# A graph layer on one core: in the gather stage the other engines wait for a drain behind each group of matmuls, and its buffers get fixed places

## The chip, the cores and the metric

The kernel runs on one core of a Trainium2 chip. A core has five engines that run side by side, each with its own queue in program order: PE (matrix multiplication), DVE (vector), ACT (scalar), POOL and SP. They tell each other of finished work by semaphores, which are counters: an instruction adds to one when it has ended, and another waits until it has reached a value. Matmuls write into PSUM, which has eight banks; everything else lies in SBUF. Transfers are done by 16 DMA engines; SP and ACT give them whole transfers, and POOL gives them gathers by an index. The metric is the time of one execution on the device in microseconds (us).

## The reference

12,500 nodes have 256 features each in `x`, and 200,000 edges go from `src` to `dst`, sorted by `dst`. Each node gets the sum of its neighbours' normalized features, two dense layers with a batch normalization each, and its own `x` back:

```python
h = jnp.maximum(_layernorm(x, axis=-1), 0.0)
agg = jax.ops.segment_sum(h[src], dst, num_segments=N)
z = (1.0 + eps_gin) * h + agg
t = jax.nn.relu(_batchnorm(jnp.dot(z, W1) + b1, g1, bt1))
out = jax.nn.relu(_batchnorm(jnp.dot(t, W2) + b2 + h, g2, bt2))
return x + out
```

Everything is float32; W1 is 256x512 and W2 512x256.

## The kernel before, in words

A short start brings the indices into columns and tests whether the fast path may be taken (lines 92 to 220). The fast path has three stages. The **gather stage** (lines 298 to 493) makes `h`, sums it over the edges and does the first layer. The second reads the first layer's result back, normalizes it and does the second layer (500 to 522). The third does the last normalization and adds `x` (527 to 549). Between stages stands the sum of a batch normalization's statistics, which needs all nodes. Only the gather stage is changed.

It works on two grids. Nodes lie in 25 chunks of 512 (`CH`), the last of 212. Edges lie in 1563 tiles of 128, in 131 groups of 12 tiles (`GT`); since edges are sorted by `dst`, the 1536 edges of a group reach fewer than 128 neighbouring nodes. The loop at line 472 takes one group per step:

- `gather(i + 4)` (377): POOL issues 12 indirect transfers (line 382), one for each tile: 128 rows of 256 features into a place `gt` of a ring of five (`AHEAD + 1`). For the first 24 groups (`LEAD`) the rows come from `x`, since `h` isn't ready, and `settle` (322) normalizes them in place on DVE and ACT (lines 328 to 339). Later ones come from the table `h_tab`. Within a group the last tile is fetched first.
- `sums(i)` (403): DVE makes one-hot matrices `oh` that say which edge belongs to which of the group's nodes (407), and PE adds up the 12 tiles in one bank `ps` with 12 matmuls (417). A float32 matmul is two passes in the profile, so a group has 24.
- `join(i - 1)` (422): ACT copies the sum of the group before out of PSUM, `zs` (424), and DVE makes a second one-hot matrix `at` that says at which columns it belongs (426).
- `put(i - 1)` (431): two matmuls (four passes) turn and place that sum in `pz` (436). `pz` has one place, two banks wide.
- `add(i - 1)` (441): DVE adds `pz` to the chunk's `zc` (449), which SP has loaded from the table `h_cols` (395) and ACT has scaled by 1 + eps (396).
- When a chunk is complete, `first_layer` (452): eight matmuls with W1, in pairs, each into a bank `ph` (458), their statistics on DVE (462) and a copy on ACT (463), which is then stored (464).

In the first 20 steps `h_chunk` (354) is called as well: it loads a chunk of `x`, normalizes it, stores it to `h_tab`, turns it with transposes on PE (365) into the bank `pc` and stores it to `h_cols`.

The order of each engine's queue is made by the framework's scheduler, from the order of the calls and its own estimates of time. Places and waits are made by it too: a pool with n buffers hands out n places in turn, and the next user of a place waits for all that used it. Each group of matmuls adds to PE's counter when its last matmul has ended, and ACT, DVE, POOL and SP wait for values of that counter: `zs` and the `oh` two groups on wait for `ps`; `add` waits for `pz`; the statistics wait for `ph`; and the first gather of a group waits for the matmuls of five groups earlier, which read the same place of the ring.

In the built program PE's queue stands so in the middle of the stage, as far as one group goes: the last ten matmuls of `ps(i)`, the first two of `ps(i+1)`, the two of `pz(i)`, the other ten of `ps(i+1)`.

Of the kernel before, what the change touches and what calls it, by code (L numbers as in the profile page):

```python
# [14 lines left out]
P = 128  # L15
# [14 lines left out]
def kernel(  # L30
# [233 lines left out]
    def fast():  # L264
# [24 lines left out]
        with ExitStack() as fs:  # L289
# [8 lines left out]
            with ExitStack() as es:  # L298
                ln = es.enter_context(tc.tile_pool(name="ln", bufs=2))
                gat = es.enter_context(tc.tile_pool(name="gat", bufs=AHEAD + 1))  # L300
                sel = es.enter_context(tc.tile_pool(name="sel", bufs=2))
                zcp = es.enter_context(tc.tile_pool(name="zc", bufs=4))
                tsp = es.enter_context(tc.tile_pool(name="ts", bufs=2))
                ps_h = es.enter_context(tc.tile_pool(name="ps_h", bufs=1, space=PSUM))
                ps_i = es.enter_context(tc.tile_pool(name="ps_i", bufs=1, space=PSUM))
                ps_s = es.enter_context(tc.tile_pool(name="ps_s", bufs=2, space=PSUM))
                ps_z = es.enter_context(tc.tile_pool(name="ps_z", bufs=1, space=PSUM))
                ps_t = es.enter_context(tc.tile_pool(name="ps_t2", bufs=2, space=PSUM))
# [13 lines left out]
                def settle(v, pairs, rows, to, tag):  # L322
# [15 lines left out]
                    for c in reversed(range(rows)):  # L338
                        nc.scalar.activation(  # L339
                            to[:, c, :], v[:, c, :], AF.Relu, bias=nb[:, c : c + 1], scale=rs[:, c : c + 1]  # L340
                        )

# [11 lines left out]
                def h_chunk(g):  # L354
# [3 lines left out]
                    ht = ln.tile([P, R, D], F32, name="ht")  # L358
                    settle(xts.pop(g), -(-slots // 2), slots, ht, "c")
                    carry(nc.scalar, ht, h_tab, g, store=True)  # L360
                    hc = ln.tile([P, DC, CH], F32, name="hc")
                    for d in range(DC):
                        ph = ps_h.tile([P, CH], F32, name="pc")
                        for c in range(slots):
                            nc.tensor.transpose(  # L365
                                ph[:, c * P : (c + 1) * P], ht[:, c, d * P : (d + 1) * P], ident
                            )
                        if d % 2:
                            nc.scalar.copy(hc[:, d, :n], ph[:, :n])
                        else:  # L370
                            nc.vector.tensor_copy(hc[:, d, :n], ph[:, :n])  # L371
                    nc.sync.dma_start(h_cols[g, :, :, :n], hc[:, :, :n])

                groups = [(t0, min(GT, NTILE - t0)) for t0 in range(0, NTILE, GT)]
                gathered = {}

                def gather(i):
                    t0, n = groups[i]
                    ga = gat.tile([P, GT, D], F32, name="gt")
                    for t in reversed(range(t0, t0 + n)):  # L380
                        rows = left if t == full_tiles else P
                        nc.gpsimd.indirect_dma_start(  # L382
                            out=ga[:rows, t - t0, :], out_offset=None, in_=x if i < LEAD else h_tab,
                            in_offset=bass.IndirectOffsetOnAxis(ap=srcT[:rows, t : t + 1], axis=0),
                        )
                    gathered[i] = ga
# [3 lines left out]
                def z_chunk(c):  # L390
# [3 lines left out]
                    zc[c] = zcp.tile([P, DC, CH], F32, name="zc")  # L394
                    nc.sync.dma_start(zc[c][:, :, :n], h_cols[c, :, :, :n])
                    nc.scalar.activation(zc[c][:, :, :n], zc[c][:, :, :n], AF.Copy, scale=gin1)
# [6 lines left out]
                def sums(i):  # L403

                    t0, n = groups[i]
                    oh = sel.tile([P, GT, P], F32, name="oh")
                    nc.vector.tensor_tensor(  # L407
# [4 lines left out]
                    )  # L412
                    ga = gathered.pop(i)
                    ps = ps_s.tile([P, D], F32, name="ps")
                    for j in range(n):
                        rows = left if t0 + j == full_tiles else P
                        nc.tensor.matmul(  # L417
                            ps, lhsT=oh[:rows, j, :], rhs=ga[:rows, j, :], start=(j == 0), stop=(j == n - 1)
                        )
                    summed[i] = ps  # L420

                def join(i):
                    zs = sel.tile([P, D], F32, name="zs", bufs=3)
                    nc.scalar.copy(zs, summed.pop(i))  # L424
                    at = sel.tile([P, WIDE], F32, name="at")
                    nc.vector.tensor_scalar(  # L426
                        at, col, shift[:, i : i + 1], None, op0=OP.is_equal
                    )
                    placed[i] = zs, at

                def put(i):

                    zs, at = placed.pop(i)
                    pz = ps_z.tile([P, DC, CH], F32, name="pz2")
                    for d in range(DC):
                        nc.tensor.matmul(  # L436
                            pz[:, d, :WIDE], lhsT=zs[:, d * P : (d + 1) * P], rhs=at, start=True, stop=True
                        )
                    return pz

                def add(i, pz):
                    lo, hi = span(i)
                    for c in range(max(lo, 0) // CH, -(-min(hi, N) // CH)):
# [5 lines left out]
                        nc.vector.tensor_add(side, pz[:, :, a - lo : b - lo], side)  # L449
                    z_chunk(max(lo, 0) // CH + 1)  # L450

                def first_layer(c):
                    n = chunks[c][1] * R
                    ts = tsp.tile([P, HC, CH], F32, name="ts")
                    for f in range(HC):
                        ph = ps_t.tile([P, CH], F32, name="ph")
                        for d in range(DC):
# [3 lines left out]
                            )  # L461
# [339 lines left out]
```

## Time and profile before

| | us |
|---|---|
| median of three runs | 2585.78 |
| lowest, highest | 2571.92, 2607.86 |
| the profiled execution | 2577.98 |
| its span, first to last instruction | 2576.2 |
| first gather's start, last gather's end | 32.45, 2275.46 |
| the second stage's first ACT instruction | 2325.12 |
| busy: PE, DVE, ACT, POOL | 1418.7, 714.3, 460.5, 1482.6 |
| mean granted clock of TensorE | 0.754 |

All further numbers come from the profiled execution. Its page has the busy time of each engine in 40 slices of the span (each digit a tenth; `PEclk` is the clock that PE was granted, in tenths of full speed). A group row gives the line, the engine, what is written from what, the number of instructions, then busy time and mean ns of one, then the idle time of the engine just before these instructions and what ended it. The list of waits gives for each waiting line what it waited for: us in all, times, longest. The timeline gives start, duration, engine, line and number of equal instructions, and in brackets the idle time before and what ended it. A row by window gives its length, then for PE, weight loads, DVE, ACT and POOL the busy time and in brackets the number, then the granted clock, the DMA engines' share and GB/s. A release is found from the semaphores' records: "remote" means that the counter moved without an instruction of this core ending just then, and "issue" that the profile shows no wait.

### The profile page before, as it was taken

The page shows a single profiled execution, that of the slowest core. Times are in us where ns is not written, and L with a number is a line of the kernel's source. Part 1 is how long each engine was busy: PE and PEld are TensorE (multiplying, and loading weights), DVE is VectorE, ACT ScalarE, POOL GpSimd, SP SyncE. Part 2 cuts the span into 40 slices and gives each one's busy share as a digit, 9 for nine tenths or more (in the row PEclk, how much of TensorE's full clock was granted, in tenths as well). Part 3 has the DMA queues.
Part 4 walks back from the last instruction along what each step waited for, and adds up shares of the span by engine and source line. Part 5 has one row for each costly group of instructions (what it writes and reads, how often), then busy time and mean ns, then how long its engine had stood idle before and what let it go on. Part 6 is the DMA issues. An engine that isn't in the chain of part 4 may idle for free.

```text
span 2576.2 us, 14802 instructions
## 1 busy us (share of the span) xinstructions
PE 1418.7 (55%) x4873; PEld 1010.7 (39%) x4873; DVE 714.3 (28%) x1060; ACT 460.5 (18%) x871; POOL 1482.6 (58%) x1575
## 2 busy tenths in 40 slices
PE   1265566545356455455545554464564555578985
PEld 1243444434244334344333443342443343353444
DVE  4355455222122112221211221221221122133444
ACT  1364566300000000000000000000000000014444
POOL 4666566666666666666666666666666666620000
PEclk6677787777678777777767777676787777788996
DMA  5566675333333333333334333333333333338539
GB/s 164 155 205 201 199 222 171 93 119 113 92 117 118 120 92 119 112 94 116 120 88 122 117 114 95 119 114 92 116 120 119 92 115 101 96 108 319 200 120 319
DMA packets 150067, 349.41 MB, mean 136 GB/s; under 512 B 28920, under 2 KB 84366, under 8 KB 143838
## 3 DMA queue, kind: packets, MB, share of 16 engines
q0 software_dynamic: 75008, 204.90, 27.4%
q1 hardware_dynamic: 44182, 91.21, 10.3%
q10 hardware_dynamic: 30792, 52.26, 5.4%
q8 instruction: 41, 0.67, 0.1%
q14 instruction: 44, 0.36, 0.0%
HBM read 284.26 MB, written 64.00 MB: 135 GB/s over the span
## 4 chain that ended last, share of the span: by engine, by line
another core or an unknown queue 49%; PE 29%; ACT 7%; issue 6%; DVE 4%; DMA 3%; SPq 0%; POOL 0%; ACTq 0%; DVEq 0%; POOLq 0%
PE ps L417 12%; PE py L517 7%; PE pz L436 5%; PE ph L458 4%; ACT gt L339 3%; DMA out_dram<-ot 1%; ACT zs L424 1%; ACT ht L339 1%; DVE oh L407 1%; DVE st L462 1%; DMA zc<-h_cols 1%; DVE zc L449 1%; PE pc L365 1%; ACT ts L463 1%
## 5 line engine op out<-in xcount | busy, mean ns | idle before, releaser
L382 POOL DMA_INDIRECT gt<-h_tab,srcT x1275 | 1207.5, 947 | 608.5 <-issue 370.9
L417 PE MATMUL ps<-gt,oh 128*128 128x256 f32 x3126 | 776.9, 409 | 55.5 <-ACT gt L339 42.8
L417 PEld LDWEIGHTS ps<-gt,oh 128*128 128x128 f32 x3126 | 654.2, 210 | 175.3 <-ACT gt L339 46.6
L436 PE MATMUL pz<-at,zs 128*128 128x280 f32 x524 | 207.2, 531 | 735.3 <-ACT zs L424 578.7
L407 DVE TENSOR_TENSOR oh<-col,dstT 128x1536 f32<-128x1536 f32 x131 | 229.0, 1748 | 1144.1 <-remote 857.0
L436 PEld LDWEIGHTS pz<-at,zs 128*128 128x128 f32 x524 | 119.4, 244 | 796.8 <-ACT zs L424 601.3
L382 POOL DMA_INDIRECT gt<-in_x_dram,srcT x288 | 273.5, 949 | 154.0 <-issue 79.9
L458 PE MATMUL ph<-zc,w1s 128*128 128x512 f32 (+1 forms) x400 | 218.2, 699 | 252.2 <-ACT ts L463 231.9
L424 ACT COPY zs<-ps 128x256 f32<-128x256 f32 x131 | 48.8, 373 | 1633.8 <-remote 1261.3
L458 PEld LDWEIGHTS ph<-zc,w1s 128*128 128x128 f32 x400 | 88.7, 230 | 362.4 <-ACT ts L463 247.0
L449 DVE TENSOR_TENSOR zc<-pz,zc 128x560 f32<-128x560 f32 (+9 forms) x203 | 100.8, 526 | 350.4 <-remote 267.6
L517 PE MATMUL py<-tT,w2s 128*128 128x512 f32 (+1 forms) x400 | 170.9, 590 | 12.0 <-ACT tT L510 12.0
L339 ACT ACTIVATE gt<-gt,nbg,rsg 128x256 f32<-128x256 f32 x288 | 149.5, 590 | 4.0 <-DVE nbg L337 1.9
L517 PEld LDWEIGHTS py<-tT,w2s 128*128 128x128 f32 x400 | 76.8, 193 | 106.0 <-issue 87.2
L462 DVE BATCH_NORM_STATS2 st<-ph 128x6 f32<-128x512 f32 (+1 forms) x100 | 66.6, 679 | 139.5 <-PE ph L458 74.8
L328 DVE BATCH_NORM_STATS2 stg<-gt 128x6 f32<-128x512 f32 x144 | 91.4, 689 | 34.2 <-DMA gt<-in_x_dram,srcT 31.2
L510 ACT ACTIVATE tT<-ti,of,sc 128x512 f32<-128x512 f32 (+1 forms) x100 | 72.0, 791 | 101.1 <-issue 86.7
L463 ACT COPY ts<-ph 128x512 f32<-128x512 f32 (+1 forms) x100 | 57.4, 575 | 181.4 <-DVE st L462 150.4
L426 DVE TENSOR_SCALAR at<-col,shift 128x280 f32<-128x280 f32 x131 | 65.4, 499 | 0.3 <-PE pz L436 0.3
L521 DVE TENSOR_TENSOR yT<-py,yT 128x512 f32<-128x512 f32 (+1 forms) x50 | 33.9, 679 | 110.5 <-PE py L517 108.5
L365 PE MATMUL pc<-ident,ht 128*128 128x128 f32 x196 | 39.2, 334 | 40.6 <-DVE hc L371 16.8
L542 PE MATMUL po<-ident,yr 128*128 128x128 f32 x196 | 40.3, 394 | 33.5 <-ACT yr L536 33.5
(74 smaller groups left out, 382.9 us busy)
## 6 DMA issues: line engine op xcount, KB each, us to landing
t_tab<-ts ACTq DMA_DIRECT2D x24, 1024.0 KB
ti<-t_tab SPq DMA_DIRECT2D x24, 1024.0 KB
gt<-h_tab,srcT POOLq DMA_INDIRECT x1275
xt<-in_x_dram SPq DMA_DIRECT2D x24, 512.0 KB
h_tab<-ht ACTq DMA_DIRECT2D x24, 512.0 KB
h_cols<-hc SPq DMA_DIRECT2D x24, 512.0 KB
zc<-h_cols SPq DMA_DIRECT2D x24, 512.0 KB
yT<-h_cols SPq DMA_DIRECT2D x24, 512.0 KB
```

Of the source, the lines that this page charges most:

```text
L328: nc.vector.bn_stats(st[:, c : c + 2, :].rearrange("p c s -> p (c s)"), v[:, c : c + 2, :].rearrange("p c d -> p d c"),)
L339: nc.scalar.activation(to[:, c, :], v[:, c, :], AF.Relu, bias=nb[:, c : c + 1], scale=rs[:, c : c + 1])
L382: nc.gpsimd.indirect_dma_start(out=ga[:rows, t - t0, :], out_offset=None, in_=x if i < LEAD else h_tab, in_offset=bass.IndirectOffsetOnAxi ...
L407: nc.vector.tensor_tensor(oh[:, :n, :], col[:, :P].unsqueeze(1).to_broadcast([P, n, P]), dstT[:, t0 : t0 + n].unsqueeze(2).to_broadcast([P ...
L417: nc.tensor.matmul(ps, lhsT=oh[:rows, j, :], rhs=ga[:rows, j, :], start=(j == 0), stop=(j == n - 1))
L424: nc.scalar.copy(zs, summed.pop(i))
L436: nc.tensor.matmul(pz[:, d, :WIDE], lhsT=zs[:, d * P : (d + 1) * P], rhs=at, start=True, stop=True)
L449: nc.vector.tensor_add(side, pz[:, :, a - lo : b - lo], side)
L458: nc.tensor.matmul(ph[:, :n], lhsT=w1s[:, d, f * P : (f + 1) * P], rhs=zc[c][:, d, :n], start=(d == 0), stop=(d == DC - 1),)
L462: nc.vector.bn_stats(st1[:, f, c, :], ph[:, :n])
L463: nc.scalar.copy(ts[:, f, :n], ph[:, :n])
L517: nc.tensor.matmul(py[:, :n], lhsT=w2s[:, f, d * P : (d + 1) * P], rhs=tT[:, f, :n], start=(f == 0), stop=(f == HC - 1),)
```

## The change

All of it lies in the gather stage. A helper puts a drain behind a list of matmuls on PE; a drain is an instruction that lets nothing behind it start before what is ahead of it on its engine has ended. The drain adds to a counter of its own. A second helper takes an instruction out of the framework's tracking against those matmuls and makes it wait for the drain:

```diff
+                def drained(matmuls):
+                    d = nc.tensor.drain()
+                    for m in matmuls:
+                        tc.add_manual_dep(d.ins, m.ins.name, NOSYNC, reason="the drain is behind it")
+                    for m in matmuls:
+                        tc.add_to_no_dep_group("pe", m.ins)
+                    return d
+
+                def behind(ins, *drains):
+                    tc.declare_no_dep(ins.ins, group="pe", reason="it waits for the drain")
+                    for d in drains:
+                        if d is not None:
+                            tc.add_manual_dep(ins.ins, d.ins.name, SYNC, reason="PE has done what it needs")
+                    return ins
```

A drain stands behind each group of `ps`, each `pz`, each pair of `ph` and each set of transposes into `pc`: 131 + 131 + 100 + 50 = 412. The readers of these results, and the next writers of what the matmuls have read, wait for the drain:

```diff
 def gather(i):
-                    ga = gat.tile([P, GT, D], F32, name="gt")
+                    ga = gt[:, i % (AHEAD + 1), :, :]
...
+                        behind(ins, added.get(i - AHEAD - 1))
 def z_chunk(c):
-                    zc[c] = zcp.tile([P, DC, CH], F32, name="zc")
-                    nc.sync.dma_start(zc[c][:, :, :n], h_cols[c, :, :, :n])
+                    zc[c] = zcs[:, c % 4, :, :]
+                    behind(nc.sync.dma_start(zc[c][:, :, :n], h_cols[c, :, :, :n]), multiplied.get(c - 4))
 def sums(i):
-                    oh = sel.tile([P, GT, P], F32, name="oh")
+                    oh = ohs[:, i % 2, :, :]
...
+                    behind(ins, added.get(i - 2))
...
+                    added[i] = drained(ms)
 def join(i):
-                    nc.scalar.copy(zs, summed.pop(i))
+                    behind(nc.scalar.copy(zs, summed.pop(i)), added[i], put_in.get(i - 3))
 def put(i):
+                    put_in[i] = drained([
 def add(i, pz):
-                        nc.vector.tensor_add(side, pz[:, :, a - lo : b - lo], side)
+                        behind(nc.vector.tensor_add(side, pz[:, :, a - lo : b - lo], side), put_in[i])
 def first_layer(c):
-                        nc.vector.bn_stats(st1[:, f, c, :], ph[:, :n])
-                        nc.scalar.copy(ts[:, f, :n], ph[:, :n])
+                        behind(nc.vector.bn_stats(st1[:, f, c, :], ph[:, :n]), multiplied[c])
+                        behind(nc.scalar.copy(ts[:, f, :n], ph[:, :n]), multiplied[c])
```

`settle` and `h_chunk` are treated alike. Since the framework no longer tracks these pairs, it can't hand out the buffers either: `gt`, `oh`, `zs`, `at`, `zc`, `ht` and the banks of `pc`, `ps`, `pz` and `ph` become one tile each, and a group takes its place by its number (`i % 2`, `i % 5` and so on). The number of places stays, but for `at`, which gets three instead of two.

The order of the built program changes a little. On PE, `pz(i)` now stands ahead of all 12 matmuls of `ps(i+1)`, with a drain ahead of it and one behind it; and where a chunk is complete, the pairs of `ph`, each with a drain behind it, stand between the matmuls of one `ps`. POOL's queue has the same gathers in the same order, with waits on the same 126 of them.

## The prediction

> **What bounds the kernel now.** Clock and span first (one core, 2576.2 us, granted TensorE clock 0.754), then busy time by slice, then who waits for whom. In the page's slices POOL works from the first slice to the 36th and ACT, after nine slices, hardly at all: the gather stage is most of the time, and POOL is its busiest engine.
>
> ```profile
> ACT  1364566300000000000000000000000000014444
> POOL 4666566666666666666666666666666666620000
> PEclk6677787777678777777767777676787777788996
> ```
>
> POOL issues 1563 gathers at a fixed pace: 947 ns busy and 0.305 us (450.8/1477) between two, 1.252 us in all. What exceeds the pace is in the two L382 groups: 608.5 + 154.0 = 762.5 us idle, less 1563 x 0.305 = 476.7, leaves **285.8 us in which POOL stands still**.
>
> ```profile
> L382 POOL DMA_INDIRECT gt<-h_tab,srcT x1275 | 1207.5, 947 | 608.5 <-issue 370.9
> L382 POOL DMA_INDIRECT gt<-in_x_dram,srcT x288 | 273.5, 949 | 154.0 <-issue 79.9
> ```
>
> ```profile
> ACT zs L424 <- remote: 1261.3, 68, 37.0
> DVE oh L407 <- remote: 857.0, 67, 22.7
> PE pz L436 <- ACT zs L424: 578.7, 57, 36.1
> POOL gt L382 <- issue: 450.8, 1477, 0.6
> POOL gt L382 <- remote: 198.2, 41, 6.4
> ```
>
> POOL stands still because a gather needs its place in the ring of five, which the matmuls of five groups earlier free. "remote" is the page's word for a release that no end of an instruction explains. ACT's `zs` copy and DVE's `oh` both wait for PE alone there. The timeline shows what that looks like:
>
> ```profile
> 1188.22 0.37 ACT L424 COPY zs<-ps 128x256 f32<-128x256 f32 x1 [7.96 <-issue]
> 1189.83 5.34 PE L417 MATMUL ps<-gt,oh 128*128 128x256 f32 x24
> ...
> 1208.92 0.95 POOL L382 DMA_INDIRECT gt<-h_tab,srcT  x1 [0.30 <-issue]
> 1214.05 0.37 ACT L424 COPY zs<-ps 128x256 f32<-128x256 f32 x1 [25.46 <-remote]
> 1214.05 1.76 DVE L407 TENSOR_TENSOR oh<-col,dstT 128x1536 f32<-128x1536 f32 x1 [22.06 <-remote]
> 1214.29 0.94 POOL L382 DMA_INDIRECT gt<-h_tab,srcT  x1 [4.42 <-remote]
> ```
>
> PE has finished that group's matmuls by 1194.3 (twenty of the x24; four belong to the next group) and then does nothing. ACT, DVE and POOL learn of it together at 1214.05, 19.7 us later and only when POOL has stood still for 4.2 us. I sorted all 131 groups by how long POOL had been issuing without a stop when the last matmul ended. Under 10 us: the copy followed within 0.5 us in 41 of 46. From 10 us on: in **0 of 61**, the median delay 16.5 us. At the end, where POOL has no more work, the delay is 0.04 to 0.09 us in each of the last five groups:
>
> ```profile
> 2274.52 0.94 POOL L382 DMA_INDIRECT gt<-h_tab,srcT  x1 [0.30 <-issue]
> 2280.31 0.37 ACT L424 COPY zs<-ps 128x256 f32<-128x256 f32 x1 [8.13 <-PE ps L417]
> 2286.44 0.37 ACT L424 COPY zs<-ps 128x256 f32<-128x256 f32 x1 [5.75 <-PE ps L417]
> 2294.17 4.48 PE L417 MATMUL ps<-gt,oh 128*128 128x256 f32 x20
> 2325.12 5.74 ACT L510 ACTIVATE tT<-ti,of,sc 128x512 f32<-128x512 f32 x8 [9.13 <-DMA ti<-t_tab]
> ```
>
> So the news that a matmul has ended is held while POOL issues steadily. The ring then runs full, POOL stops, and that stop lets the news through. Nobody's work is the bound; a lock-step is.
>
> **The change, part by part.**
>
> *Who is waited for.* In the stage every wait on a matmul becomes a wait on a drain: 412 drains, 131 behind `ps`, 131 behind `pz`, 100 behind `ph`, 50 behind the transposes. In the order of the changed program no ACT, DVE, POOL or SP instruction of the stage waits on a matmul's own count, so it does what it says. Whether a drain's count is prompt the trace cannot show: it has none in the stage. Bounds: 0.04 us, as matmuls have with POOL idle, and 16.5 us, as they have now. I take the prompt end: ACT's and DVE's counts, made in the same stretches, are prompt (`zs` ends at 1214.43, `pz` starts at 1214.48), so what is held is PE's matmul completion and not the waiting engines.
>
> *What that is worth.* (a) The stops: 285.8 us. Of these, 61 lie between 110 and 480 us, where each group also needs 12 normalizations on ACT. By busy time nothing binds there: in 370 us and 20.6 groups ACT has 212.4 (10.3 a group), PE 227.8 (11.1), DVE 188.8 (9.2), against 15.0 of POOL. But PE also waited 35.7 us there for ACT `gt` L339. I leave 20 us of stops, somewhat over half of that; bounds 0 and 61. Gain 265.8. (b) The end: now 49.7 us pass from the last gather's end (2275.46) to the first `tT` (2325.12), since PE is four groups behind. If it keeps up, only the last two remain: from `ps` at 2294.17 to 2325.12 are 31 us, and these can start about when the last gather ends. Gain 19, taken as 20. Bounds 0 and 25.
>
> *What the drains cost PE.* A drain holds back what stands behind it on PE until the pipe is empty. The nearest row: the last matmul of group 62 starts at 1187.81 and ACT, waiting for it, starts at 1188.22, so 0.4 us; the lower end is 0. With restart I take 0.5, and 3.15 drains a group make 1.6 us.
>
> *What is moved.* `pz` now stands ahead of all of the next group's `ps`; before, two of those matmuls filled the wait for `zs`. That costs 0.37 + 0.1 = 0.5 us a group, and the matmuls of the first layer now stand in pairs between those of `ps`. PE is busy 927.4 us in the 105 groups from 480 to 2280:
>
> ```profile
> 480.00:2280.00 1800.00, 927.39 (x3258) 690.60 (x3259) 362.10 (x456) 112.39 (x216) 1194.27 (x1261) 0.74 0.36 109
> ```
>
> 8.8 + 1.6 + 0.5 = 10.9 us a group, under POOL's 15.02. So 4.1 us of POOL cover it, and if that cover goes, 105 us come on the path for each us a group that exceeds it.
>
> *Fixed places.* The ring of five, the two `oh`, three `zs`, four `zc` and the banks keep their numbers (`at` gets three instead of two). Their waits become explicit; those of POOL stand on the same 126 gathers. SP's `zc` loads wait, as before, for the use four chunks earlier, over 40 us away, with nothing urgent behind them. ACT still scales `zc` ahead of `zs` (48.8 us of waits for that load in the whole run, in 17 waits up to 3.3), about 0.4 us a group under the same cover. I cost them at nothing, bounds -5 and +10.
>
> **Sum.** 2577.98 (the profiled execution; its span and 1.8 us around it; 0.3% under the median 2585.78 and inside the runs' 2571.92 to 2607.86) - 265.8 - 20 = **2292 us**.
>
> The Trainium skill has a rule against this change (PSUM — Partial Sum Buffer, "Engine vs sequencer instructions"): put the increment on the matmul itself, because it fires at completion, while a drain waits for the engine to go fully idle. By that rule nothing is late, the drains are mere cost, and the time stays at 2578 or above. The 0 of 61 speaks otherwise. Another page (Perfetto Trace Analysis, "Per-engine timelines") says that a matmul's count is pushed when PSUM acknowledges the write and a sequencer instruction's by the sequencer. No run shown here tells if the second way is free.
>
> **The rivals.**
>
> *Held all the same.* If it is the completion that is late, or every count from PE, a drain is late too and blocks PE besides. For it: the trace has no prompt count from PE in a long POOL run. Against it: the delay ends with POOL's stops, though POOL never touches PSUM in this program. Its price turns on one point: after each restart PE must end the next group's `ps` before POOL has issued for 10 us. Now it does at 8.0, with two matmuls done ahead. Those add four passes of 0.43, and two drains 0.2 to 1.0: 9.9 to 10.7. If it still fits, two groups pass per stop as now: 2578. If not, each group of 15.0 pays a stop of 4.3, 19.3 instead of 17.1: 105 x 2.2 = 231 more, **2810**.
>
> *PE becomes the bound.* The counts come promptly, but the granted clock falls to a half. Then `pz` takes 2.2 us (row of 1214.48), 24 passes 10.3, the first layer 16 x 0.86 / 5.24 = 2.6, with 2.1 for drains and wait 17.2 a group: 2.2 over POOL, 2292 + 231 = 2523. Against it: today's bursts start at half clock and are at full clock some 5 us on, and the slices show 0.7 on average.
>
> *Partly.* The first 480 us and the end gain nothing, and each group loses a little: 2292 + 41 + 20 = 2353, and up to 2480 with 1.2 us a group.
>
> **How the numbers follow.** Prompt and covered 0.58 (its own range 2265 to 2335: with all stops gone and 25 at the end 2267; with 61 us of early stops 2333); partly 0.08; PE bound 0.06; held, two groups a stop 0.10 (2560 to 2640); held, one a stop 0.16; others slower 0.02. The range that leaves out 2 in 10 runs from 2262 to 2640. A measurement tells about 2% from no change: faster 0.58 + 0.08 = 0.66; same 0.06 (PE bound) + 0.07 of the 0.10 held at two groups a stop = 0.13; slower the rest, 0.03 + 0.16 + 0.02 = 0.21.
>
> **What would show it.** Right: POOL's gathers in runs without stops, `zs` released within 0.5 us of the last matmul in any group, its "remote" waits gone, POOL's last gather near 2010 us, PE busy about 11 of each 15 us. Wrong: `zs` or `oh` released together with POOL after a stop (held); POOL stopping while PE is busy all the time at a clock near 0.5 (PE bound); a wait of `zs` on ACT's own queue in its place.

## The result, and the profile after

The changed kernel is **slower**: 2689.45 us median of four runs (2680.78 to 2716.05) against 2595.2 us of the kernel before (four runs, 2571.92 to 2607.86), a ratio of 1.039 with a 95% interval of 1.028 to 1.050. The profiled execution has a span of 2684.7 us at a granted clock of 0.771. The forecast was 2292 us.

Each ratio below compares runs made on one and the same chip; on some chips the kernel before takes about 2600 us, as above, and on others about 2271 us, and each experiment says which.

Line numbers of the changed kernel: `zs` is now L460, `ps` L452, `oh` L440, `pz` L473, `add` L487, `ph` L496, `st` L501, `ts` L502, the gathers L411, and every drain is L334. The two groups of POOL's gathers, on the page of the changed kernel's groups by line (busy us, mean ns of one, then idle time before them and what ended it):

```profile
L411 POOL DMA_INDIRECT gt<-h_tab,srcT x1275 | 1208.9, 948 | 672.2 <-issue 364.9 <-PEq L334 290.2 <-ACT zss L460 13.2
L411 POOL DMA_INDIRECT gt<-in_x_dram,srcT x288 | 273.7, 950 | 189.7 <-issue 60.2 <-ACT zss L460 42.1 <-PEq L334 41.8
```

The pace of the gathers is unchanged (948 ns, 0.305 us between two). Their idle time grew from 762.5 to 861.9 us. Less the pace (1563 times 0.305 us, 476.7 us), **POOL now stands still for 385 us instead of 286**. What ended most of its stops was "remote" and is now "PEq L334", a drain. The last gather ends at 2376.8 instead of 2275.5, which is 101 of the 108 us by which the span grew.

The waits of the changed kernel:

```profile
ACT zss L460 <- PEq L334: 1446.2, 102, 38.4
DVE ohs L440 <- PEq L334: 1234.6, 121, 23.9
...
POOL gt L411 <- PEq L334: 331.9, 67, 15.5
```

The same lines wait as before, and longer: `zs` 1446 us where it had 1261, `oh` 1235 where it had 857. The drains themselves, as the view of line 334 has them (duration in ns: least, median, longest), and one of the largest pieces of the chain that ended last (start and length in us):

```profile
L334 PEldq DRAIN  x412: 13/2415/42108, 44.5 to 2422.2; - x138
```

```profile
1154.65 23.56 PEldq L334
```

The same place on the timeline:

```profile
1151.35 0.37 ACT L460 COPY zss<-pss 128x256 f32<-128x256 f32 x1 [3.81 <-PEq L334]
...
1153.07 5.44 PE L452 MATMUL pss<-gt,ohs 128*128 128x256 f32 x24
...
1173.11 0.95 POOL L411 DMA_INDIRECT gt<-h_tab,srcT  x1 [0.30 <-issue]
1178.24 0.37 ACT L460 COPY zss<-pss 128x256 f32<-128x256 f32 x1 [26.51 <-PEq L334]
1178.24 1.76 DVE L440 TENSOR_TENSOR ohs<-col,dstT 128x1536 f32<-128x1536 f32 x1 [23.90 <-PEq L334]
1178.47 0.95 POOL L411 DMA_INDIRECT gt<-h_tab,srcT  x1 [4.41 <-PEq L334]
```

All 24 passes of the group are done at 1158.51. The drain behind them ends at 1178.2, when POOL has stood still for 4.4 us, and ACT, DVE and POOL go on together. This is the picture of before with the drain in the place of "remote".

I sorted the drains as the prediction sorted `zs`, by how long POOL had issued without a stop when the last matmul ahead of the drain ended. Under 10 us, 202 of 223 drains end within 0.5 us of that matmul. From 10 us on it is **12 of 100, with a median of 5.7 us and up to 36**. For the copy `zs` alone, which the prediction counted, it is 0 of 47 with a median of 16.5 us: what it was before (0 of 61, 16.5). A limit holds for all such delays: the profile computes the end of a matmul and does not observe it. So the traces do not tell whether the matmul's work ends late or only PE's notice of it.

### The profile page after: what moved, and what is told of

Its sections match the earlier page's. It is cut to its first block, busy times and chain, and to the rows that moved or that the text cites. A ratio compares the mean times of both kernels' runs of the same rounds, so it can differ in the third digit from the quotient of the medians.

```text
span 2684.7 us, 15533 instructions
## 1 busy us (share of the span) xinstructions
PE 1507.9 (56%) x4873; PEld 990.0 (37%) x4873; DVE 719.7 (27%) x1060; ACT 459.3 (17%) x871; POOL 1484.2 (55%) x1575
## 4 chain that ended last, share of the span: by engine, by line
PEldq 32%; issue 26%; PEld 16%; PE 7%; POOL 5%; DMA 4%; ACT 3%; DVE 2%; DVEq 0%; ACTq 0%; SPq 0%
PEldq L334 32%; PEld pss L452 12%; PE py L556 6%; POOL gt L411 5%; PEld pzs L473 2%; PEld phs L496 2%; DMA out_dram<-ot 2%; DMA gt<-h_tab,srcT 1%; ACT gt L365 1%; ACT zss L460 1%; DVE st L501 1%; ACT ts L502 0%; DVE ot L587 0%; DMA zcs<-h_cols 0%; PEld pcs L392 0%
## 5 line engine op out<-in xcount | busy, mean ns | idle before, releaser
L411 POOL DMA_INDIRECT gt<-h_tab,srcT x1275 | 1208.9, 948 | 672.2 <-issue 364.9
L452 PE MATMUL pss<-gt,ohs 128*128 128x256 f32 x3126 | 819.3, 420 | 165.5 <-issue 119.4
L452 PEld LDWEIGHTS pss<-gt,ohs 128*128 128x128 f32 x3126 | 641.1, 211 | 387.8 <-issue 240.1
L440 DVE TENSOR_TENSOR ohs<-col,dstT 128x1536 f32<-128x1536 f32 x131 | 229.1, 1749 | 1268.0 <-PEq L334 1234.6
L473 PE MATMUL pzs<-ats,zss 128*128 128x280 f32 x524 | 208.7, 533 | 546.2 <-ACT zss L460 499.4
L496 PE MATMUL phs<-zcs,w1s 128*128 128x512 f32 (+1 forms) x400 | 235.4, 719 | 267.1 <-issue 257.9
L411 POOL DMA_INDIRECT gt<-in_x_dram,srcT x288 | 273.7, 950 | 189.7 <-issue 60.2
L473 PEld LDWEIGHTS pzs<-ats,zss 128*128 128x128 f32 x524 | 114.2, 242 | 637.7 <-ACT zss L460 532.4
L460 ACT COPY zss<-pss 128x256 f32<-128x256 f32 x131 | 48.9, 373 | 1492.9 <-PEq L334 1446.2
L496 PEld LDWEIGHTS phs<-zcs,w1s 128*128 128x128 f32 x400 | 89.1, 233 | 347.5 <-issue 330.5
L501 DVE BATCH_NORM_STATS2 st<-phs 128x6 f32<-128x512 f32 (+1 forms) x100 | 68.6, 686 | 321.8 <-PEq L334 281.9
L487 DVE TENSOR_TENSOR zcs<-pzs,zcs 128x560 f32<-128x560 f32 (+9 forms) x203 | 101.0, 527 | 122.1 <-PEq L334 89.5
L502 ACT COPY ts<-phs 128x512 f32<-128x512 f32 (+1 forms) x100 | 57.6, 576 | 415.2 <-DVE st L501 357.6
L462 DVE TENSOR_SCALAR ats<-col,shift 128x280 f32<-128x280 f32 x131 | 65.4, 500 | 0.0
```

The costliest lines, as they stand in the source:

```text
L411: ins = nc.gpsimd.indirect_dma_start(out=ga[:rows, t - t0, :], out_offset=None, in_=x if i < LEAD else h_tab, in_offset=bass.IndirectOffse ...
L440: ins = nc.vector.tensor_tensor(oh[:, :n, :], col[:, :P].unsqueeze(1).to_broadcast([P, n, P]), dstT[:, t0 : t0 + n].unsqueeze(2).to_broadc ...
L452: ms.append(nc.tensor.matmul(ps, lhsT=oh[:rows, j, :], rhs=ga[:rows, j, :], start=(j == 0), stop=(j == n - 1)))
L460: behind(nc.scalar.copy(zs, summed.pop(i)), added[i], put_in.get(i - 3))
L473: nc.tensor.matmul(pz[:, d, :WIDE], lhsT=zs[:, d * P : (d + 1) * P], rhs=at, start=True, stop=True) for d in range(DC)
L487: behind(nc.vector.tensor_add(side, pz[:, :, a - lo : b - lo], side), put_in[i])
```

## The experiments

Theory when they were begun (A): PE itself does not see its matmuls as ended while POOL issues gathers for long; a drain waits for that, and blocks PE's queue besides. Rivals: the new order or the places cost the time (B), or only the count is late on its way to others (C).

### Taking the drains out again, and heeding them not

e1 leaves places and order as changed and lets everybody wait for the count of a group's last matmul; e2 is the same with the drains put back, for which nobody waits.

```diff
 def drained(matmuls):                       # e1
-    d = nc.tensor.drain()
...
-    return d
+    for a, b in zip(matmuls, matmuls[1:]):
+        tc.add_manual_dep(b.ins, a.ins.name, NOSYNC, reason="the one is behind the other")
+    for m in matmuls[:-1]:
+        tc.add_to_no_dep_group("pe", m.ins)
+    return matmuls[-1]
```

Expected of e1: 

> The changed kernel (fixed places, order written out) with the matmul counts of before in place of the drains: every wait of the stage is on the count of a group's last matmul, and there is no drain. Theory A (the drains are what makes the changed kernel slower: PE does not see its own matmuls as ended while POOL issues, and a drain makes PE's queue wait for that): about the time of before, 2560 to 2640 us, with POOL's stops near 286 us in some 72 stops, as before. Rival B (the drains are innocent, the new order or the places cost the time: pz ahead of all ps, first layer in pairs): about the time of the changed kernel, 2660 to 2720 us.

Expected of e2: 

> The same, with the 412 drains put back behind the groups of matmuls, but nobody waits for them: all waits stay on the matmul counts. Theory A (PE itself does not see the end of its matmuls): the drains are as long as in the changed kernel (some 1970 us in sum, median near 7 us where POOL has issued for 10 us or more), PE's queue stands behind them, and the time is that of the changed kernel, 2650 to 2730 us. Rival C (only the count is late on its way from PE to the other engines, and a drain's long record is its own count on its way): the drains end within 1 us nearly everywhere, and the time is that of the kernel before with 1 to 2 us of drains a group hidden, 2560 to 2640 us.

Measured: e1 2692.78 us, ratio 1.038 (1.031 to 1.045), POOL's stops 382 us. **Theory A falls as far as the sum goes: without any drain the loss is the same**, and rival B's number is met. e2 took 2696.43 us, 1.038 (1.031 to 1.044). Its drains carry no count at all, and their records are as long as in the changed kernel:

```profile
L334 PEldq DRAIN  x412: 13/2785/39733, 43.3 to 2434.3; - x138
```

In long POOL runs 27 of 114 end within 0.5 us of the last matmul, the median is 4.8 us and the longest delay 34.9 us. A drain without a count has nothing to send to anybody. And nobody waits for these drains, yet where the count of a `ps` is held (38 groups with POOL issuing for 10 us or more), `zs`, which waits for the matmul's own count, starts within 0.1 us of the drain's end in 24 and 0.7 to 1.4 us ahead of it in the other 14. So rival C falls too: PE itself does not see the matmuls as ended. Theory A's mechanism is shown, but the drains are not needed for the 3.9%.

Where the loss comes from without drains, e1's timeline shows (POOL's steady gathers left out):

```profile
929.18 1.88 PE L495 MATMUL phs<-zcs,w1s 128*128 128x512 f32 x4
...
930.90 1.89 PE L451 MATMUL pss<-gt,ohs 128*128 128x256 f32 x8
...
941.15 0.70 DVE L500 BATCH_NORM_STATS2 st<-phs 128x6 f32<-128x512 f32 x1 [10.56 <-remote]
941.88 0.59 ACT L501 COPY ts<-phs 128x512 f32<-128x512 f32 x1 [13.05 <-issue]
...
942.52 3.38 PE L495 MATMUL phs<-zcs,w1s 128*128 128x512 f32 x4 [9.73 <-ACT ts L501]
...
951.67 3.30 PE L495 MATMUL phs<-zcs,w1s 128*128 128x512 f32 x4 [4.04 <-ACT ts L501]
...
954.76 1.02 PE L451 MATMUL pss<-gt,ohs 128*128 128x256 f32 x2
...
956.05 0.94 POOL L410 DMA_INDIRECT gt<-h_tab,srcT  x1 [9.82 <-PE pss L451]
```

In the changed order the four pairs of a chunk's first layer stand between the matmuls of one `ps`. The bank of a pair is free only when ACT's copy `ts` of the pair two earlier is done. That copy follows DVE's statistics `st`, which wait for a held count ("remote", 10.56 us). The last matmuls of `ps`, which free POOL's place, wait behind it on PE: POOL stops for 9.8 us instead of 4. e1 has twelve stops of 8 to 12 us after the first 480 us ("late" below), at groups 34, 45, 50, 55, 82, 87 and so on, in the rhythm of the chunks (512 nodes are 5.3 groups); before has none.

### Trying to end the hold

e3 and e4 change the kernel before on POOL alone: in e3 each gather waits for the landing of the gather three back, in e4 a fill of one column stands behind every sixth gather.

```diff
+ tc.add_manual_dep(issued[-1].ins, issued[-4].ins.name, SYNC, reason="few under way")   # e3
+ if count[0] % 6 == 0: nc.gpsimd.memset(speck, 0.0)                                     # e4
```

Expected of e3: 

> The kernel before, with each gather waiting for the landing of the gather three back instead of the one eight back: at most three of POOL's gathers are under way or queued. Theory D (the hold comes from the depth of POOL's queue: it begins after some 8 gathers, 10 us, and eight are let ahead): the matmul ends are no longer held, POOL's stops shrink from 286 us to 20 to 60, and the time is 2290 to 2380 us. Rival E (the hold comes from steady issuing as such, whatever the depth): a gather lands about 2.5 us after its start, so the wait costs a pace of 1.25 us nothing or some tenths; held as before, 2570 to 2700 us.

Expected of e4: 

> The kernel before, with a tiny fill of one column on POOL behind every sixth gather of both gather paths' fast one (261 fills). Theory F (an unbroken row of more than 8 gathers on POOL brings the hold; other work on POOL between them ends it): zs follows the last matmul within 0.5 us at any length of POOL's run, the stops go, 2300 to 2400 us. Rival E (steady issuing of gathers, in whatever company): held as before, the time grows by what the fills cost POOL, 261 x 0.1 to 0.3 us = 26 to 80 us at most and partly taken from the stops: 2560 to 2670 us.

Measured: e3 2607.28 us, 1.001 (0.998 to 1.004); e4 2609.47 us, 1.003 (1.000 to 1.006). In long POOL runs `zs` was prompt in 4 of 63 (e3) and 0 of 62 (e4). Theories D and F fall: neither a queue of some eight gathers nor an unbroken row of them is what holds the counts. But e3 changed little of what was under way. In the kernel before, where POOL stops for over 3 us, the last DMA packet of the last gather ends 2.4 us after that gather's start (3.4 at most), so at 1.25 us a gather no more than three were under way there either. Fewer than three was not tried.

### The first layer put together, without and with drains

e5 is e1 with the pairs of `ph` in a row, ahead of `pz` and of the next `ps`; e6 is the changed kernel, drains and all, with the same.

```diff
+ layered[0] = ms[-1]                       # the last matmul of the pair
...
+ tc.add_manual_dep(m.ins, layered[0].ins.name, NOSYNC, reason="the layer is ahead")   # for each matmul of ps and pz
```

Expected of e5: 

> The kernel of e1 (fixed places, matmul counts, pz ahead of the next ps) with one thing put back: the eight matmuls of a chunk's first layer stand together on PE, behind a whole ps and ahead of pz, as they about do before; no ps matmul stands between them. Theory G (the loss sits in the first layer: in e1 its four pairs stand between the ps matmuls, the third pair waits for a bank whose copy waits for a held count, and the ps matmuls behind it, which POOL needs, wait along; e1 has eleven stops of about 10 us late in the stage, at 34, 45, 50, 55, 82, 87 ... groups, that is at chunks): the 10 us stops go, POOL's late stops fall from 280 to about 220 us, 2600 to 2640 us (the early 36 us remain). Rival H (the loss sits in pz standing ahead of all of ps, or in the places): the time stays at 2670 to 2700 us.

Expected of e6: 

> The changed kernel, drains and all, with the same one thing put back. Theory G, with drains that cost nothing of their own: as e5, 2600 to 2640 us. Rival I (drains that block PE's queue cost besides: the next ps can't run ahead during a hold): 30 to 80 us above e5, 2640 to 2720 us.

Measured: e5 2660.37 us, **1.016** (1.007 to 1.025); one late stop of 8 to 12 us is left of twelve, late stops are 254 us instead of 280 (before: 217). By the medians theory G holds for over half of e1's loss, though less came back than expected, and e1 ran on another chip. e6 2726.08 us, **1.039** (1.031 to 1.048): rival I holds, the drains cost 2.4 points of their own as soon as the order is mended. It has thirteen stops of 8 to 12 us, again at the chunks. One of them on e6's timeline (the drains behind its last three pairs end at 930.16, 934.39 and 942.80):

```profile
931.64 1.98 PE L507 MATMUL phs<-zcs,w1s 128*128 128x512 f32 x4 [2.74 <-ACT ts L515]
...
935.87 2.54 PE L507 MATMUL phs<-zcs,w1s 128*128 128x512 f32 x4 [2.25 <-issue]
942.87 2.23 PE L481 MATMUL pzs<-ats,zss 128*128 128x280 f32 x4 [4.46 <-issue]
...
947.11 7.25 PE L458 MATMUL pss<-gt,ohs 128*128 128x256 f32 x24 [2.02 <-issue]
...
954.65 0.94 POOL L417 DMA_INDIRECT gt<-h_tab,srcT  x1 [11.69 <-PEq L334]
```

Each pair now passes its own drain before the next may start; the four pairs and `pz` take from 923 to 945, and `ps` only then begins. So some 2.4 points of the loss have two sufficient causes that do not add: pairs that wait for each other's copies between the `ps` matmuls, or pairs that wait at drains ahead of them. Take out one, and the other still makes it; with both out, 1.6% are left (e5).

How the two meet in the changed kernel itself is not shown. Its late stops are 65 of 283 us where before has 54 of 217, only three of them longer than 8 us (12.2 to 13.0, at groups 93, 109 and 125): there are more stops of the usual size rather than long ones at the chunks. And a third of what its stops grew by lies in the first 480 us (102 us instead of 69), which no run takes apart.

### What on POOL holds the counts

e7 fetches rows of half the width with as many gathers. e8 replaces each gather by a plain load of 128 consecutive rows through the same queue.

```diff
- in_=h_tab, out=ga[:rows, t - t0, :]
+ in_=h_tab.rearrange("n (a p) -> (n a) p", p=P), out=ga[:rows, t - t0, :P]              # e7
...
- nc.gpsimd.indirect_dma_start(...)
+ nc.gpsimd.dma_start(ga[:rows, t - t0, :], (x if i < LEAD else h_tab)[r0 : r0 + rows, :])   # e8
```

Expected of e7: 

> The kernel before, where the gathers from h_tab fetch rows of half the width (512 bytes from a table seen as twice as many rows; ps takes the half twice): as many gathers on POOL, half the bytes; it leaves out half of the gathered data. Theory J (the bytes on the way bring the hold): it weakens, many zs prompt, 2350 to 2500 us. Rival K (POOL's issuing brings it, whatever the bytes): zs prompt in none of the long runs, POOL's pace 1.25 us as before, 2540 to 2620 us.

Expected of e8: 

> The kernel before, where each gather is a plain load of 128 consecutive rows through the same queue of POOL: it leaves out the gathering, the data are other rows. Theory L (the indirect gather on POOL brings the hold): no hold, POOL's issues shorter, the stage is bound by PE or the loads, below 2400 us. Rival M (any transfer whose descriptors POOL makes brings it): held in long runs as before, with stops of the same 4 us.

Measured: e7 2600.17 us, 0.994 (0.990 to 0.999), and `zs` prompt in 0 of 65: rival K, the bytes do not bring the hold. e8 **1419.33 us**, 0.541 (0.535 to 0.546). POOL's issue and ACT's wait in e8:

```profile
L383 POOL DMA_DIRECT2D gt<-h_tab x1275 | 674.7, 538 | 136.8 <-PE ps L417 102.5 <-issue 20.7 <-ACT zs L424 6.9
```

```profile
ACT zs L424 <- PE ps L417: 545.1, 112, 6.1
```

"remote" is gone; `zs` follows within 0.5 us in 46 of 46 cases in which POOL had issued for 10 us or more. Theory L holds: on this chip, where the kernel before held its counts (2620.34 us), the same bytes through the same queue hold nothing when they are not gathered by an index. With the index went the scattered rows and 0.41 us of POOL's time for each transfer (0.538 us instead of 0.947); which of these matters was not tried.

### PE's order as before, and blocks of groups

e9 is e5 with two matmuls of the next `ps` ahead of `pz`, so that PE's queue is nearly that of before. e10 to e12 try what the lock-step suggests: since a count comes at a stop of POOL, let more groups pass one stop. PE takes three or four groups' `ps` in a row, with the `pz` of the block before ahead of them.

```diff
+ pz, late = put(ahead, ms[1])                                                    # e9, in sums, behind two matmuls
...
+ for b0 in range(0, NG + BLOCK, BLOCK):                                          # e10 to e12
+     for i in range(max(b0 - BLOCK, 0), min(b0, NG)): join(i)
...
- col = ps_i.tile([P, WIDE], F32, name="col")                                     # PSUM
+ col = keep.tile([P, WIDE], F32, name="col")                                     # SBUF
```

Expected of e9: 

> The kernel of e5 (fixed places, matmul counts, the first layer together) with the other thing put back as well: two matmuls of the next group's ps stand ahead of pz on PE, as before. If what e5 still loses (1.6%, some 40 us) comes from pz standing ahead of all of the next ps, the time is that of before within 0.7%, 2590 to 2625 us. If it comes from the fixed places or from the order on ACT in the first 24 groups, it stays at 2640 to 2680 us.

Expected of e10: 

> A new order with matmul counts, fixed places and the ring of five: PE takes three groups' ps in a row, and the pz of the three groups before stand ahead of them, with one pair of the first layer behind each; oh, zs, at and the banks of ps have three places each or more (col moves from PSUM to SBUF, zc gets five places). Theory N (a count from PE is passed on only at a stop of POOL and in some 10 us behind it, so what counts is how many groups pass a stop): three groups of 15.0 us and one stop of 4 to 5 make 16.5 us a group in place of 17.1; 107 groups by 0.6 are 64 us: 2520 to 2570 us. Rival O (the hold is not the lock: PE or the work behind a stop is): the time stays at 2600 us or, with the three pz and the pairs of the layer in a row behind each stop, rises to 2650 to 2750.

Expected of e11: 

> The same with four groups in a block. Theory N: four groups of 15.0 and one stop make 16.1 to 16.3 us a group: 2490 to 2540 us. It turns at one point: behind a stop four pz with their adds, about 1.7 us each, and three to four pairs of the first layer must end within the 10 us in which counts still come; if they do not, the last pz waits for the next stop with all of ps behind it, and each block pays two stops, one of them with the rest of four groups of ps: above 2650 us.

Expected of e12: 

> The same with a ring of six places instead of five. Theory N: a sixth place lets POOL go on for one group while the block's counts are held, so a stop falls once per four to five groups at best, 15.9 to 16.2 us a group, 2470 to 2540 us; and if the window behind a stop is too short, it is so here too.

Measured: e9 2644.72 us, 1.014 (1.005 to 1.022): `pz` ahead of `ps` is not what e5 still loses (late stops 258 us, in e5 254). e10 2671.09 us, 1.028 (1.019 to 1.038); e11 2680.95, 1.030 (1.021 to 1.038); e12 2656.77, 1.020 (1.012 to 1.028). The numbers of theory N fail, its mechanism does not: POOL has 33 stops of 213 us in all in e10 (before: 73 of 285, counted stop by stop). The gain was lost elsewhere, as POOL's group row and timeline of e10 show:

```profile
L416 POOL DMA_INDIRECT gt<-h_tab,srcT x1275 | 1325.7, 1040 | 545.2 <-issue 381.7 <-remote 107.6 <-PE pss L457 51.9
```

```profile
1297.02 1.76 DVE L445 TENSOR_TENSOR ohs<-col,dstT 128x1536 f32<-128x1536 f32 x1 [24.53 <-remote]
1297.26 2.34 POOL L416 DMA_INDIRECT gt<-h_tab,srcT  x1 [8.11 <-remote]
1299.08 1.76 DVE L445 TENSOR_TENSOR ohs<-col,dstT 128x1536 f32<-128x1536 f32 x1 [0.29 <-PE pss L457]
1299.90 1.74 POOL L416 DMA_INDIRECT gt<-h_tab,srcT  x1 [0.30 <-issue]
```

A gather takes 1.040 us on average instead of 0.947, because 116 of them in the stage take 1.5 to 2.5 us, and each of the 116 overlaps an `oh` of DVE (e11 has 91 such gathers, e12 96). `oh` compares `col` with `dstT`; to free a bank I had moved `col` from PSUM to SBUF, and so both inputs lay in SBUF. In before, the changed kernel, e1, e5 and e9, with `col` in PSUM, no gather of the stage but the very first (1.6 us) is longer than 0.97 us. The 116 cost 139 us, twice what the stops had given. The Trainium skill says so too (GPSIMD Engine Reference, "Key points"): POOL shares its SBUF interfaces with DVE and collides with DVE instructions that have two inputs in SBUF; the trace agrees and gives the price.

### The same where nothing is held

e13 gives `at` two places again on top of e9 (then DVE's queue is that of before as well), e14 and e15 are e10 and e11 with `col` back in PSUM, e16 is the changed kernel with the plain loads of e8.

```diff
- ats = own.tile([P, 3, WIDE], F32, name="ats")
+ ats = own.tile([P, 2, WIDE], F32, name="ats")                                   # e13
```

Expected of e13: 

> The kernel of e9 with two places for at instead of three. With three, DVE's queue has at (0.50 us) ahead of the add of the group before; with two it has the add first, as before the change. If that half microsecond behind each stop is what the changed kernel loses besides the first layer (e9 has 258 us of late stops against 220), some 30 us come back: 2595 to 2625 us, within 0.7% of before. If the fixed places themselves cost it, it stays at 1.0 to 1.7% above.

Expected of e14: 

> e10 (three groups of ps in a block, ring of five) with col back in PSUM, where before has it. In e10 the stops fell from 285 to 213 us, but 118 gathers lasted 2.4 us instead of 0.95, each of them beside an oh that DVE makes; that took 140 us. If the place of col is the reason (oh with all operands in SBUF against oh with one in PSUM), the long gathers go and so do these 140 us: 2510 to 2560 us, faster than both kernels. If it is the order of the blocks, they stay: 2650 to 2680 us.

Expected of e15: 

> e11 (four groups in a block) with col back in PSUM, in the same way. e11 had 93 long gathers worth 112 us and stops of 234 us. If the place of col is the reason: 2540 to 2580 us; if not, 2660 to 2690 us.

Expected of e16: 

> The changed kernel with each gather as the plain load of e8 (128 consecutive rows through the same queue of POOL; it leaves out the gathering). e8 showed no held count, and 1419 us with the matmul counts. Theory P (the plain price of the drains, with nothing held, is small and was estimated about right: 0.5 us each, 412 of them, 206 us where PE is the bound): 1500 to 1640 us, and every drain shorter than some 1.5 us. Rival Q (drains are long by themselves, 2.4 us in the median as in the changed kernel): 412 by 2.4, 2000 us or more.

Measured: on this chip the kernel **before takes 2271.39 us**. e13 2283.17, 1.005 (1.003 to 1.006); e14 2283.43, 1.005 (1.004 to 1.007); e15 2288.82, 1.008 (1.006 to 1.009). POOL issues from 33 to 1987 us without a stop (e15 has one, of 1.4 us), and the counts are prompt all the same: in e13 `zs` follows within 0.5 us in 123 of 129 cases. The long gathers are gone in e14 and e15, in which over 200 gathers overlap an `oh`. The chip changed along with the place of `col`; but with `col` in PSUM there are none on the first chips either (e9), so the place of `col` is the reason as far as these runs go. What the blocks are worth in the lock-step could not be seen here, and neither could the part of `at`. e16 took 1568.03 us, 0.690 (0.689 to 0.692): theory P's time, though not its drains of 1.5 us; their records have a median of 1.8 us, but all of them end within 0.14 us of the last matmul ahead. e16 less e8 is 149 us for 412 drains and the new order (on two chips, neither run with a held count), 0.36 us for each drain.

e17 repeats e13, and e18 the changed kernel itself.

Expected of e17: 

> The kernel of e13 once more, since in that call no count was held, in the kernel before neither (2271 us there, POOL without a stop), and so nothing of the lock-step could be seen. Where the kernel before stands near 2600 us again: if the at ahead of the add (0.50 us) is what e9 still loses, within 0.7% of before; if the fixed places cost it, 1.0 to 1.7% above, as e9. Where the kernel before stands near 2271 us again, 0.3 to 0.7% above it, as in e13.

Expected of e18: 

> The changed kernel itself once more, beside the kernel before. In the last two calls the kernel before took 2271 us, on another chip each time, and no count was held; in the three calls ahead of them, and where the result was taken, it took about 2600 and counts were held. Theory R (the loss is the hold and what stands in PE's queue behind it; without a hold the drains lie beside POOL's work, as the prediction's sum had it): where the kernel before takes 2271 us, the changed one takes 2270 to 2310, POOL without a stop. Rival S (the drains or the order cost it by themselves): 2340 us or more there. Where the kernel before takes about 2600 us, both expect 2660 to 2720 us.

Measured: the kernel before again took 2271.51 and 2270.82 us, on two further chips. e17 2283.22 us, 1.005 (1.004 to 1.006). e18, the changed kernel, **2280.28 us, 1.004** (1.002 to 1.005): theory R. In e18, POOL's larger group, the view of the drains, and the timeline of about the same 27 us as above:

```profile
L411 POOL DMA_INDIRECT gt<-h_tab,srcT x1275 | 1205.3, 945 | 388.4 <-issue 378.6 <-PEq L334 4.0 <-ACT gt L365 2.4
```

```profile
L334 PEldq DRAIN  x412: 13/1923/5743, 44.5 to 2012.8; - x138
```

```profile
1151.55 0.37 ACT L460 COPY zss<-pss 128x256 f32<-128x256 f32 x1 [4.73 <-PEq L334]
...
1159.63 7.58 PE L452 MATMUL pss<-gt,ohs 128*128 128x256 f32 x24 [6.44 <-DMA gt<-h_tab,srcT]
1167.27 0.37 ACT L460 COPY zss<-pss 128x256 f32<-128x256 f32 x1 [15.35 <-PEq L334]
...
1174.57 6.95 PE L452 MATMUL pss<-gt,ohs 128*128 128x256 f32 x24 [5.67 <-DMA gt<-h_tab,srcT]
```

The same program, gather for gather: now `ps` waits for its data, not for a count, `zs` follows 0.06 us behind the last pass (1167.21), and from 60 us on all drains of the stage, 409, end within 0.16 us of their matmuls. A drain's record still has a median of 1.9 us, since it begins when PE's queue reaches it, with matmuls ahead of it still running: its length alone says nothing, only the time from the last matmul's end to its own.

## Why the prediction was wrong, point by point

- **What bounds the kernel** (a lock-step of held matmul ends and stops of POOL): right. The stops account for the loss in the changed kernel as they did for the time before, and where nothing is held the kernel before takes 2271 us, close to 2578 less the 286 us of stops and the end's 20. One reading went too far: not every count waits for a stop. Of the 61 held `zs`, 48 start in a stop of POOL and 13 when it has been issuing for 20 to 31 us.
- **"I take the prompt end"** is the step that failed. A drain's count was bounded by 0.04 and 16.5 us, and 0.04 was taken. In long POOL runs it is 12 of 100 within 0.5 us and 5.7 us in the median, and 16.5 us for `zs`. The reason given was half right: what is held is PE's matmul completion and not the waiting engines. (The instance given for it, `pz` at 1214.48, lies at POOL's restart at 1214.29, where PE's counts are prompt too. e1's timeline above shows it in a long run: ACT's `ts` ends at 942.47 and PE goes on at 942.52, with POOL issuing since 916.44.) But a drain waits for exactly that completion, so the reason spoke for the other end. The first rival had said so: "a drain is late too and blocks PE besides"; e2 shows it with drains that carry no count.
- **(a) The stops, -265.8**: +99. **(b) The end, -20**: +10; from the last gather's end to the first `tT` it takes 59.6 us instead of 49.7, since PE is still four groups behind and each now needs 7.2 us instead of 6.1. The 7.2 against 6.1 is what the drains and the moved `pz` cost with POOL idle: 1.1 us a group, where two drains and `pz` were put at 1.5.
- **"The matmuls of the first layer now stand in pairs between those of `ps`"** was seen, and costed with 0.5 us for `pz` under POOL's cover. That cover exists only if nothing is held. In the lock-step, without drains, the position is worth 2.2 points of e1's 3.8 (e1 against e5, by the medians, on two chips). The working had the wait, not what stood in line behind it: a pair waits for a copy that waits for a held count, and POOL's place waits behind the pair.
- **The rival "held all the same"** was the case, between its two prices (2578 with two groups a stop, 2810 with one): from group 24 on, the runs of POOL between stops are 42 of two groups and 22 of one, where before had 12 of three, 28 of two and 14 of one.
- **Places at nothing, -5 to +10**: with nothing held, e13 and e17 have places and nearly the order of before and lose 12 us. In the lock-step 1.4% are left in e9; whether DVE's `at` ahead of `add` or the places make it stays open, since e13 and e17 ran where it cannot be seen.
- **The rest of the sum** was sound: where no count is held, the changed kernel takes 2280 us, against 2292 forecast. Only, the change does not bring that about; the chip or its condition does, for the kernel before too.
- **The skill's rule** against the change (PSUM — Partial Sum Buffer, "Engine vs sequencer instructions") had the sign. The page offers the drain as a barrier that waits for the engine to go idle; here it gained nothing, cost 2.4 points in e6 against e5, and taken out alone gave nothing back (e1). Its other half, that the increment on the matmul fires at completion, is not contradicted: it was the completion that PE saw late.

What in a chip makes the hold stays open. It was there with gathers by an index and gone with plain loads (e8), there on some chips and not on others; half the bytes (e7), a limit of three gathers (e3) and a broken row (e4) did not end it. No version was faster than the kernel before on its chip with all the work done. e14, with e10's stops and no long gathers, would by e10's profiled run (the fastest of its four) be near 2654.7 - 138.9 = 2516 us where counts are held. That is an estimate, at the low end since POOL may stop for part of what it saves, and was not run there.

## What to carry to other kernels

When a completion is seen late, ask which engine sees it late before choosing another way to report it: the drains here, on the same engine, ended as late as the counts came. In a lock-step, do not cost an instruction by its duration but by what stands in line behind it until the next release. And where a kernel moves an operand between PSUM and SBUF to free room, count it as a change to the engines that share the path.

## What the runs showed of the hardware

- On three chips (and where the result was taken) the kernel before took 2572 to 2636 us, with `zs` prompt in 0 of 61 cases (in its trace) once POOL had gathered for 10 us. On three others it took 2270 to 2274 us, and in the traces taken there (e13, e17, e18) counts are prompt though POOL issues for 1950 us in one run. The second sort came later than the first, so whether it is the chip or its condition at the time is not told apart. Two kernels that differ by 3.9% on the first sort differ by 0.4% on the second.
- On a chip of the first sort PE itself sees the ends of matmuls up to 36 us late (the changed kernel's drains) while POOL issues gathers by an index, and not while it issues plain loads of the same size.
- A gather on POOL (0.947 us) takes up to 2.5 us beside a DVE comparison with both inputs in SBUF, and 0.97 at most beside the same with one in PSUM (the first gather of the stage, 1.6 us, left aside).
